# Graph layer 1 of a four-layer kernel: attention times tokens first, then times W

## The chip, the cores and the metric

The kernel runs on one core of one Trainium2 chip. The metric is the device time of one execution in microseconds (us), taken as the median over the runs. The core has four engines that compute and run side by side: TensorE (PE in the profile; its weight loads are PEld), VectorE (DVE), ScalarE (ACT) and GpSimd (POOL). SyncE (SP) issues the transfers. Every engine works through its own list of instructions in order and waits, by semaphores, for what it needs. All data are 32-bit floats unless said otherwise.

## The reference, cut to what matters

There are 64 graphs of 256 nodes with 256 features each, `x` of 64 x 256 x 256, and an adjacency matrix `adj` of 0 and 1 for each graph. Four layers follow one another; each normalises its input, applies ReLU, runs one kind of graph layer, and adds the outcome to `x`. Layer 0 is attention with eight heads, layer 2 three steps of a gated recurrent unit, layer 3 graph attention with four heads. The change is in layer 1, a graph attention with one head whose softmax runs over the rows (axis 1):

```python
h = jnp.maximum(_layernorm(x, axis=-1), 0.0)
Wh = jnp.einsum('bnf,fo->bno', h, W)
a1 = a[:fout, 0]
a2 = a[fout:, 0]
f1 = Wh @ a1
f2 = Wh @ a2
e = f1[:, :, None] + f2[:, None, :]
e = jnp.where(e >= 0, e, ALPHA * e)
attention = jnp.where(attn_mask > 0, e, MASK_FILL)
attention = jax.nn.softmax(attention, axis=1)
h_prime = jnp.einsum('bij,bjo->bio', attention, Wh)
x = x + jax.nn.elu(h_prime)
```

Two identities are used below: `attention @ (h @ W)` equals `(attention @ h) @ W`, and `(h @ W) @ a1` equals `h @ (W @ a1)`.

## The kernel before, in words

**Tiling.** Two graphs make a pair, so there are 32 pairs. A pair's `x` is one tile of 128 partitions by 4 x 256: the four token tiles `t` (two for each graph `g`) stand behind each other in a partition. Large working tiles have the tag `w4`, half as long ones `w2`, the eight accumulator banks `ps`; `part` are tiles of 512 elements for layer 2, and `mask` holds masks in bf16. A name in the profile such as `w` or `ps` is the tag without its number.

**Order.** The code of the layers does not issue instructions. It describes tasks with `add(...)`: on which engine (or on which of two), for how many us by the writer's estimate, which tiles are read and written, and the code to issue. `Plan.order` (lines 135 to 220) then goes through all tasks of all pairs and picks, again and again, the one that can begin first by those estimates. Ties are settled by a key: the pair's number times `PERIOD`, plus a number from the table `KEYS` by stage and engine (line 150). It also gives out the buffers; each tag has a count and a number of spares in `SLOTS` (line 265), and a task of a pair other than the oldest may not take the last spares. So several pairs are under way at once, and one pair's matrix products fill the time in which another pair waits. Products that use a part of the array ("rows", "columns", "halves") are kept together where possible. The outcome is a fixed order on each engine.

**Normalisation.** `norm_relu_T` (line 517) takes statistics on VectorE (L525, L527), the inverse root on GpSimd (L538, L539), and normalises four token tiles with ScalarE (L552) or VectorE (L558). It then turns the result with eight 128x128 transposes on TensorE (L577), four to a bank, and evicts each bank with ReLU, on ScalarE (L589) or VectorE (L590). The turned tile `hT` has features on the partitions. Layer 2 also needs the tokens upright, so it applies ReLU before the transposes, always on ScalarE.

**Layer 1** (`layer1`, line 834). The matrix `w1a` holds W and, in two more columns, W times the two halves of `a` (made once in `weights1`, line 395, with eight records at L406). For each token tile two products of 258 columns (L848) give `Wh` and both scores; VectorE copies the two score columns to `f12` (L852) and ScalarE the rest to `wh` (L855). `to_all` (line 813) transposes the f1 column to a row (L817), stores it and loads it into all partitions. ScalarE adds f2 and applies the leaky ReLU (L863); VectorE adds the mask, which a transfer has turned (L871), and takes the row's extreme (L688); ScalarE takes exp with its sum (L890). `wh` is divided by the sums (L896 or L900), and the products L913 of `e` with `wh`, 256 columns wide, give the outcome. ELU and the addition to `x` follow (L925 to L935). A product of 32-bit floats in the code is two records, each a weight load and a matmul, in the profile.

**Around it.** Layer 2's 24 gate products of 512 columns for each step (L1010) take most of TensorE's time. Its three message steps use `part` tiles: two masks are kept for the pair (L945), and each message product (L987) reads a high part (L971, L972) and a low part (L977). The fused mask row `lowered` (L688) is used by layers 0, 1 and 3. `evict` (L354 on ScalarE, L355 on VectorE) copies a bank to a tile. `turn` (L642) and `turn_chunks` (L663) turn tiles through a VectorE transpose of 32x32 blocks and transfers; the latter is used after each step of layer 2 for all pairs but the last.

Of the kernel before, what the change touches and what calls it, by code (L numbers as in the profile page):

```python
# [9 lines left out]
FP = mybir.dt.float32  # L10
# [29 lines left out]
class Plan:  # L40
# [18 lines left out]

    PERIOD = 1901  # L60


    KEYS = {
        ("io", "SP"): -29236, ("w", "SP"): 6718, ("w", "on"): -18369, ("w", "PE"): 8658, ("0n", "on"): -3731,
        ("0n", "SP"): 6915, ("0n", "PE"): 4357, ("0", "on"): 15591, ("0", "PE"): -6774, ("0s", "PE"): -16165,
        ("0s", "on"): 28734, ("0e", "on"): 12526, ("0e", "SP"): 43331, ("0c", "PE"): -12002, ("0c", "on"): 78735,
        ("1n", "on"): 783, ("1n", "SP"): -19498, ("1n", "PE"): -22885, ("1", "on"): -14680, ("1", "PE"): -13623,
        ("1r", "PE"): -1967, ("1r", "on"): -21520, ("1r", "SP"): -32647, ("1e", "on"): 1478, ("1c", "PE"): -9889,
        ("1c", "on"): -20145, ("2n", "on"): -1930, ("2n", "SP"): 38894, ("2n", "PE"): 5230, ("2", "on"): -6722,
        ("2h", "PE"): 9451, ("2h", "on"): -282, ("2m", "on"): -7288, ("2m", "PE"): 3883, ("2r", "PE"): 8501,  # L70
        ("2r", "on"): -21450, ("2u", "PE"): 9616, ("2u", "on"): 5167, ("2z", "PE"): 9836, ("2z", "on"): -13574,
        ("2b", "on"): 6539, ("2b", "SP"): 9757, ("3n", "on"): 23011, ("3n", "SP"): 30321, ("3n", "PE"): -1821,
        ("3", "on"): -11142, ("3", "PE"): -62749, ("3r", "on"): -37804, ("3r", "PE"): -7201, ("3r", "SP"): 18532,
        ("3e", "on"): 30365, ("3e", "SP"): 3733, ("3c", "PE"): 856, ("3c", "on"): 16925, ("3b", "on"): -30583,
        ("3b", "SP"): 12452, ("out", "SP"): -66168, ("2b", "PE"): 67575, ("3e", "PE"): -99949, ("3b", "PE"): 59983,
    }
# [147 lines left out]
def tile_adj_preln_d4(  # L224
# [42 lines left out]
        "w4": (24, [P, T * D], FP, 5),  # L267
        "part": (12, [P, N2], FR, 0),
        "f3": (2, [P, T, E3], FP, 0),
        "mask": (5, [P, T * N], BF, 0),  # L270
        "ps": (8, [P, 512], FP, 2),
        "w2": (3, [P, N2], FP, 2),
        "st": (4, [P, T, 6], FP, 1),
        "mv": (4, [P, T, 2], FP, 0),
        "rs": (4, [P, 2, T], FP, 2),
        "mx": (16, [P, H0], FP, 5),
        "zs": (12, [P, H0], FP, 7),
        "rz": (12, [P, H0], FP, 1),
        "f12": (2, [P, 2, T], FP, 1),
        "rows": (3, [T * H3, P], FP, 1),  # L280
        "dst": (4, [P, T, H3], FP, 3),
        "turn": (8, [P, T * N], FP, 3),
        "turn2": (4, [P, N2], FP, 1),
        "row1": (4, [N2], FP, 0),
        "row3": (4, [H3 * N2], FP, 3),
    }
# [10 lines left out]
    def held(name, shape):  # L297
        return const.tile(shape, FP, name=name)

    wq_sb, wk_sb, wv_sb, wo_sb = [held(name, [P, 2, D]) for name in ("wq_sb", "wk_sb", "wv_sb", "wo_sb")]  # L300
    bo_bc = held("bo_bc", [P, D])
    w1a = held("w1a", [P, 2, D + 2])
    w3a = held("w3a", [P, 2, E3])
# [91 lines left out]
    def weights1():  # L395

        load_w(w1a[:, :, 0:D], w1, W1)
        load(lambda: a1_sb.rearrange("p w k -> p (w k)"), a1.rearrange("(c p) e -> p (c e)", p=P), (W1, "a"))
        w1T = w4()
        turned(lambda o: w1a[:, o, 0:D], (0, 1), (0, 1), lambda: w1T()[:, 0:N2], (W1, w1T, [w1T]))  # L400
        ps = bank()

        def product():
            for f in range(2):
                for k in range(2):
                    mm(  # L406
                        ps()[:, 2 * f : 2 * f + 2], w1T()[:, k * D + f * P : k * D + (f + 1) * P], a1_sb[:, :, k],
                        start=k == 0, stop=k == 1,
                    )

        add((PE, 0.5, product), reads=[w1T, W1], writes=[ps])
        add(
            (V, 0.1, lambda: nc.vector.tensor_copy(w1a[:, :, D : D + 2], ps()[:, 0:4].rearrange("p (f w) -> p f w", w=2))),
            reads=[ps], writes=[W1],
        )

# [94 lines left out]


    def by_dma(l, p):

        return p < B // 2 - 1

    def norm_relu_T(xt, p, tokens=False):

# [29 lines left out]
        for g in range(2):  # L548
# [16 lines left out]
            else:  # L565
                forms = [(V, 0.7, scaled_v, True), (A, 1.0, lambda f=scaled: f(AF.Identity))]
            add(forms, reads=[(xt, g), (mv, g), (rs, g)], writes=[(xn, g)])
        hT = w4()
        hT.fine = fine
# [29 lines left out]

    def wide(hT, k):  # L600
        return tok(hT(), N2)[:, k]

    def graph_mm(ps, src, rhs, g, ):
# [53 lines left out]
    def turn_chunks(src, dst):  # L657
# [12 lines left out]
        dst.mixed = True  # L670

    def by_block(ap):
        return ap.rearrange("p (b n) -> p b n", b=4)
# [27 lines left out]
    def layer0(xt, p):  # L701
        at, hT = norm_relu_T(xt, p)
        mb = buf("mask")
# [130 lines left out]
    def layer1(xt, p):  # L834
        at, hT = norm_relu_T(xt, p)
        m1 = buf("mask")
        add(
            (V, dve2(T * N), lambda: nc.vector.tensor_scalar(
                m1(), at().bitcast(I32), 0.0, MASKED, ALU.is_le, ALU.mult), True),
            reads=[at, hT], writes=[m1],  # L840
        )
        wh, f12 = w4(), buf("f12")
        for t in range(T):
            ps = bank()

            def product(t=t, ps=ps):
                for k in range(2):
                    mm(ps()[:, 0 : D + 2], chunk(hT, k, t), w1a[:, k, :], start=k == 0, stop=k == 1)  # L848

            add((PE, 0.88, product), reads=[hT, W1], writes=[ps], claims=[wh, f12])  # L850
            add(
                (V, 0.07, lambda t=t, ps=ps: nc.vector.tensor_copy(f12()[:, :, t], ps()[:, D : D + 2])),  # L852
                reads=[ps], writes=[(f12, t)],
            )
            add((A, act(D), lambda t=t, ps=ps: nc.scalar.copy(tok(wh())[:, t, :], ps()[:, 0:D])), reads=[ps], writes=[(wh, t)])  # L855
        f1 = buf("w2")
        plan.stage = "1r"
        to_all(buf("row1"), f12, lambda: f12()[:, 0], T, [f1])
        e = w4()
        for t in range(T):  # L860
# [15 lines left out]
        for g in range(2):  # L876
# [17 lines left out]
            def divided(g=g):  # L894
                for t in (2 * g, 2 * g + 1):
                    nc.scalar.mul(tok(wh())[:, t, :], tok(wh())[:, t, :], rz()[:, t : t + 1])  # L896

            add(
                [
                    (V, dve(N2), lambda two=two: nc.vector.tensor_tensor(  # L900
                        tok(wh())[:, two, :], tok(wh())[:, two, :], rz()[:, two].unsqueeze(2).to_broadcast([P, 2, D]), ALU.mult), True),
                    (A, 2 * act(N, 1), divided),
                ],
                reads=[(rz, g)], writes=[(wh, 2 * g), (wh, 2 * g + 1)],
            )
        plan.stage = "1c"
        for g in range(2):
            ps, ex = bank(), buf("w2")

            def product(g=g, ps=ps):  # L910
                for ci in range(2):
                    for cj in range(2):
                        mm(  # L913
                            ps()[:, ci * D : (ci + 1) * D],
                            tok(e(), N)[:, 2 * g + cj, ci * P : (ci + 1) * P],
                            tok(wh())[:, 2 * g + cj, :],
                            start=cj == 0,
                            stop=cj == 1,
                        )

            parts = [(b, 2 * g + c) for b in (e, wh) for c in range(2)]
            add((PE, 1.76, product), reads=parts, writes=[ps], claims=[ex])

# [16 lines left out]
    def layer2(xt, p):  # L940
        at, hT, h = norm_relu_T(xt, p, tokens=True)
        ams = [buf("part") for g in range(2)]
# [56 lines left out]
        for l in range(NL):  # L999
# [44 lines left out]
            for o in range(2):  # L1044
                ps = gate(1.72, ((giT[:, l], aT),), (4 + o) * P, o, [u])
                add(
                    (V, dve(N2), lambda o=o, ps=ps, hn=hn: nc.vector.tensor_add(at_o(hn, o), ps(), at_o(hn, o))),  # L1047
                    reads=[ps], writes=[(hn, o)],
                )
                add(  # L1050
                    (A, act(N2, 1), lambda o=o, hn=hn: nc.scalar.activation(  # L1051
                        at_o(hn, o), at_o(hn, o), AF.Tanh, bias=bih_sb[:, 4 + o : 5 + o])),
                    writes=[(hn, o)],
                )
                add(
                    either(0.0, lambda eng, o=o, u=u, hT=hT, hn=hn: eng.tensor_sub(at_o(u, o), at_o(hT, o), at_o(hn, o))),  # L1056
                    reads=[(hT, o), (hn, o)], writes=[(u, o)],
                )
# [21 lines left out]
            plan.stage = "2b"  # L1080
            if by_dma(l, p):
                turn_chunks(u, h)
# [24 lines left out]
    def layer3(xt, p):  # L1107
        at, hT = norm_relu_T(xt, p)
        mb = buf("mask")
# [192 lines left out]
```

## Time and profile before

| | |
|---|---|
| median of 3 runs | 3577.19 us (3577.04 to 3578.66) |
| the profiled execution | 3574.28 us, its span 3572.5 us |
| TensorE busy | 3520.7 us |
| VectorE busy | 2802.2 us |
| ScalarE busy | 2614.9 us |
| GpSimd busy | 454.3 us |
| granted TensorE clock, mean | 0.995 |
| transfers | 687.72 MB, 193 GB/s |

A row of a group names the line, the engine, the operation, what is written and read with its shape, and the count; behind the bar stand the busy time of the group, the mean time of one in ns, and the idle time of the engine just before these instructions with what ended it. Matmuls overlap and their ends are modelled: a mean of 277 ns is not what one costs in a row of many, which is read from the starts in a listing by time. A row of waits gives the total in us, how often, and the longest.

### The profile page before, as it was taken

The numbers are of one execution on the slowest core, as the hardware profiler recorded it, in microseconds if no ns is written. First come the engines' busy times: TensorE is split into PE (matmuls) and PEld (weight loads), VectorE is DVE, ScalarE is ACT, GpSimd is POOL, SyncE is SP. The second block draws the span as 40 slices with busy tenths as digits, with TensorE's granted clock in tenths as the row PEclk, the third lists the DMA queues.
The fourth block names the chain that finished last, engine by engine and source line by source line (L and its number), as shares of the span: only waits on it lengthen the run. The fifth ranks groups of instructions, "written<-read, shape, count | busy, mean of one in ns | idle before, by whom it ended". The sixth has DMA issues, their size and how long they took to land.

```text
span 3572.5 us, 54870 instructions
## 1 busy us (share of the span) xinstructions
PE 3520.7 (99%) x15601; PEld 1990.1 (56%) x15601; DVE 2802.2 (78%) x8499; ACT 2614.9 (73%) x7012; POOL 454.3 (13%) x509
## 2 busy tenths in 40 slices
PE   8999999999999999999999999999999999999997
PEld 5565555555555555555555555555555555555554
DVE  7887687887778887788877878877888778878665
ACT  7796476877777777777867767876788767878555
POOL 2001111101111110111101111111111111111000
PEclk9999999999999999999999999999999999999998
DMA  8774487776767767677667767667687676786633
GB/s 232 205 207 133 130 235 202 205 197 181 207 183 221 207 180 200 190 220 201 195 183 196 223 183 212 190 191 212 180 224 199 180 198 187 210 223 180 169 107 118
DMA packets 544144, 687.72 MB, mean 193 GB/s; under 512 B 86113, under 2 KB 463073, under 8 KB 543841
## 3 DMA queue, kind: packets, MB, share of 16 engines
q1 hardware_dynamic: 543840, 684.21, 68.3%
q8 instruction: 125, 2.05, 0.3%
q14 instruction: 179, 1.46, 0.1%
HBM read 394.28 MB, written 281.35 MB: 189 GB/s over the span
## 4 chain that ended last, share of the span: by engine, by line
PE 82%; ACT 7%; DVE 6%; DMA 3%; issue 1%; SPq 1%; POOL 1%; DVEq 0%; ACTq 0%; POOLq 0%
PE ps L1010 45%; PE ps L719 6%; PE ps L607 6%; PE ps L987 4%; PE ps L740 3%; PE ps L1128 3%; PE ps L848 3%; PE ps L577 3%; PE ps L1183 3%; PE ps L792 2%; PE ps L913 2%; ACT w L695 2%; ACT w L1160 1%; DVE w L642 1%; DMA x<-in_x_dram 1%; DVE w L688 1%
## 5 line engine op out<-in xcount | busy, mean ns | idle before, releaser
L1010 PE MATMUL ps<-w,whhT 128*128 128x512 f32 x2304 | 1076.7, 595 | 0.3 <-ACT w L354 0.2
L1010 PE MATMUL ps<-w,giT 128*128 128x512 f32 x2304 | 1070.9, 593 | 0.0
L695 ACT ACTIVATE w<-w,mx 128x256 f32<-128x256 f32 x1536 | 758.9, 499 | 18.5 <-DVE mx L688 17.9
L1010 PEld LDWEIGHTS ps<-w,giT 128*128 128x128 f32 x2304 | 434.0, 190 | 526.2 <-issue 509.9
L1010 PEld LDWEIGHTS ps<-w,whhT 128*128 128x128 f32 x2304 | 423.4, 190 | 454.5 <-issue 426.1
L354 ACT COPY w<-ps 128x512 f32<-128x512 f32 x519 | 291.1, 581 | 307.0 <-PE ps L719 90.6
L642 DVE STREAM_TRANSPOSE w<-w 128x1024 f32<-128x1024 f32 x380 | 469.6, 1236 | 43.6 <-ACT w L695 21.8
L688 DVE CUSTOM_DVE_ANT_0 w<-ps,mask 128x256 f32<-128x256 f32 x1024 | 370.6, 416 | 124.2 <-PE ps L740 124.0
L695 ACT ACTIVATION_READ_ACCUMULATOR w<-w,mx 128x1 f32 x1536 | 294.8, 192 | 0.0
L538 POOL TENSOR_SCALAR rs<-mv 128x4 f32<-128x4 f32 x129 | 41.2, 319 | 1973.8 <-DVE mv L527 1953.9
L772 ACT ACTIVATE w<-w,rz 128x256 f32<-128x256 f32 x606 | 266.2, 501 | 2.2 <-DVE rz L765 2.1
L552 ACT ACTIVATE w<-x,rs 128x256 f32<-128x256 f32 x396 | 208.1, 592 | 54.5 <-DVE rs L544 52.3
L1064 ACT ACTIVATE w<-ps,brz 128x512 f32<-128x512 f32 x192 | 129.9, 677 | 156.3 <-PE ps L1010 156.3
L1034 ACT ACTIVATE w<-ps,brz 128x512 f32<-128x512 f32 x192 | 130.1, 678 | 147.6 <-PE ps L1010 147.3
L987 PE MATMUL ps<-part,part 128*128 128x256 f32 x1536 | 222.2, 298 | 9.7 <-DVE part L945 4.9
L1056 POOL TENSOR_TENSOR w<-w,w 128x512 f32<-128x512 f32 x87 | 111.8, 1285 | 909.5 <-ACT w L1051 540.4
L1160 ACT ACTIVATE w<-w,f 128x256 f32<-128x256 f32 x512 | 220.3, 499 | 4.6 <-DMA w<-row 4.5
L987 PEld LDWEIGHTS ps<-part,part 128*128 128x128 f32 x1536 | 195.7, 193 | 42.0 <-issue 23.7
L1051 ACT ACTIVATE w<-w,bih_sb 128x512 f32<-128x512 f32 x192 | 136.4, 717 | 102.6 <-DVE w L1047 101.7
L525 DVE BATCH_NORM_STATS2 st<-x 128x6 f32<-128x256 f32 x512 | 189.7, 412 | 25.4 <-DMA x<-in_x_dram 23.5
L1069 DVE SCALAR_TENSOR_TENSOR w<-w,w 128x512 f32<-128x512 f32 x192 | 136.3, 710 | 92.3 <-ACT w L1064 90.3
L688 DVE CUSTOM_DVE_ANT_0 w<-w,mask 128x256 f32<-128x256 f32 x512 | 197.7, 426 | 8.5 <-ACT w L1160 8.2
(114 smaller groups left out, 5129.4 us busy)
## 6 DMA issues: line engine op xcount, KB each, us to landing
turn<-w SPq DMA_DIRECT2D x473, 512.0 KB
w<-turn SPq DMA_DIRECT2D x1892, 128.0 KB
w<-in_adj_dram SPq DMA_DIRECT2D x128, 512.0 KB
w<-row SPq DMA_DIRECT2D x64, 512.0 KB
x<-in_x_dram SPq DMA_DIRECT2D x64, 256.0 KB
out_dram<-x SPq DMA_DIRECT2D x64, 256.0 KB
turn<-w SPq DMA_DIRECT2D x62, 256.0 KB
w<-turn SPq DMA_DIRECT2D x248, 64.0 KB
```

The lines of the kernel that those rows point to most:

```text
L354: (A, act(n), lambda: nc.scalar.copy(dst(), src())),
L525: nc.vector.bn_stats(st()[:, t, :], tok(xt())[:, t, :])
L552: nc.scalar.activation(tok(xn())[:, t, :], tok(xt())[:, t, :], func, bias=rs()[:, 1, t : t + 1], scale=rs()[:, 0, t : t + 1])
L607: mm(ps()[:, c * D : (c + 1) * D], chunk(src, k, 2 * g + c), rhs[:, k, :], start=k == 0, stop=k == 1)
L642: add((V, dve(T * N), lambda: nc.vector.transpose(blocks(), blocks())), writes=[e])
L688: nc.vector.tensor_tensor_reduce(row, src, mask, scale, 3.0e38, ALU.add, ALU.min, mn)
L695: nc.scalar.activation(row(e, r), row(e, r), AF.Exp, bias=mn()[:, r : r + 1], scale=-1.0, accum_out=zs()[:, z0(r) : z0(r) + 1])
L719: mm(ps(), w[:, k, o * P : (o + 1) * P], wide(hT, k), start=k == 0, stop=k == 1)
L772: op(row, row, rz()[:, r : r + 1])
L987: mm(ps()[:, o * N : (o + 1) * N], chunk_of(part(), h.mixed, c, o), tok(ams[g](), N)[:, c, :], start=i == 0 and c == 0, stop=i == 1 and c ...
L1010: mm(ps(), w[:, k, c0 : c0 + P], wide(src, k), start=n == 0, stop=n == 2 * len(terms) - 1)
L1160: nc.scalar.activation(dst, src, AF.Prelu, bias=f()[:, t, D + h : D + h + 1], alpha=ALPHA)
```

## The change: what it does, and the diff

Layer 1 no longer turns its normalised tokens: the function, now `norm_relu`, stops after the normalisation with ReLU on ScalarE and returns upright tokens `h`. W times the halves of `a` is made once as two rows of 256, the same in all partitions (`wa_bc`); the scores are eight fused multiply-and-add rows for a pair on VectorE, which write `f12` directly and use `e` for their products. `h`, in place of `wh`, is divided by the sums of the softmax. The attention is multiplied with `h` first; that sum is evicted to `u`, and `u` is multiplied with W. ELU and the addition are as before. All keys, `PERIOD` and several counts of buffers and spares are new: `part` goes from 12 tiles to 10, `w2` from 3 to 4. `by_dma` is asked with a stage now; with `TURNED` as it stands it holds after each step of layer 2, as before, and for none of the four normalisations, so `turn_rows` is not called. The subtraction at L1056 reads and writes what it did.

```diff
-    PERIOD = 1901
+    PERIOD = 2008
     KEYS = {
-        ("io", "SP"): -29236, ("w", "SP"): 6718, ("w", "on"): -18369, ("w", "PE"): 8658, ("0n", "on"): -3731,
+        ("io", "SP"): -22628, ("w", "SP"): 6160, ("w", "on"): -16051, ("w", "PE"): 28184, ("0n", "on"): -19306,
...
-        "part": (12, [P, N2], FR, 0),
+        "part": (10, [P, N2], FR, 1),
-        "w2": (3, [P, N2], FP, 2),
+        "w2": (4, [P, N2], FP, 1),
...
-        add((PE, 0.5, product), reads=[w1T, W1], writes=[ps])
+        add((PE, 1.72, product), reads=[w1T, a_w], writes=[ps])
+        add(evict(N2, lambda: wa_bc.rearrange("p w f -> p (w f)"), ps), reads=[ps], writes=[(W1, "b")])
...
+    TURNED = ("2m",)
     def by_dma(l, p):
-        return p < B // 2 - 1
+        return l in TURNED and p < B // 2 - 1
...
+        if not turning:
+            plan.stage = base
+            return at, xn
...
     def layer1(xt, p):
-        at, hT = norm_relu_T(xt, p)
+        at, h = norm_relu(xt, p, tokens=True, turning=False)
...
-        wh, f12 = w4(), buf("f12")
-        for t in range(T):
-            ps = bank()
-            def product(t=t, ps=ps):
-                for k in range(2):
-                    mm(ps()[:, 0 : D + 2], chunk(hT, k, t), w1a[:, k, :], start=k == 0, stop=k == 1)
-            add((PE, 0.88, product), reads=[hT, W1], writes=[ps], claims=[wh, f12])
-            add(
-                (V, 0.07, lambda t=t, ps=ps: nc.vector.tensor_copy(f12()[:, :, t], ps()[:, D : D + 2])),
-                reads=[ps], writes=[(f12, t)],
-            )
-            add((A, act(D), lambda t=t, ps=ps: nc.scalar.copy(tok(wh())[:, t, :], ps()[:, 0:D])), reads=[ps], writes=[(wh, t)])
+        e, f12 = w4(), buf("f12")
+        for g in range(2):
+            def dots(g=g):
+                for t in (2 * g, 2 * g + 1):
+                    for w in range(2):
+                        nc.vector.tensor_tensor_reduce(
+                            tok(e(), N)[:, t, :], tok(h())[:, t, :], wa_bc[:, w, :], 1.0, 0.0, ALU.mult, ALU.add, f12()[:, w, t : t + 1])
+            add(
+                (V, 4 * FUSED, dots, True), reads=[(h, g), W1], writes=[(e, 2 * g), (e, 2 * g + 1), (f12, g)],
+            )
...
-            ps, ex = bank(), buf("w2")
-            def product(g=g, ps=ps):
-                for ci in range(2):
-                    for cj in range(2):
+            psu, ps, u, ex = bank(), bank(), buf("w2"), buf("w2")
+            def sums(g=g, psu=psu):
+                for k in range(2):
+                    for c in range(2):
                         mm(
-                            ps()[:, ci * D : (ci + 1) * D],
-                            tok(e(), N)[:, 2 * g + cj, ci * P : (ci + 1) * P],
-                            tok(wh())[:, 2 * g + cj, :],
-                            start=cj == 0,
-                            stop=cj == 1,
+                            psu()[:, k * N : (k + 1) * N],
+                            tok(h())[:, 2 * g + c, k * P : (k + 1) * P],
+                            tok(e(), N)[:, 2 * g + c, :],
+                            start=c == 0,
+                            stop=c == 1,
                         )
-            add((PE, 1.76, product), reads=parts, writes=[ps], claims=[ex])
+            add((PE, 1.74, sums), reads=[(h, g), (e, 2 * g), (e, 2 * g + 1)], writes=[psu], claims=[u])
+            add(evict(N2, u, psu), reads=[psu], writes=[u])
+            def product(u=u, ps=ps):
+                for c in range(2):
+                    for k in range(2):
+                        mm(
+                            ps()[:, c * D : (c + 1) * D], u()[:, k * N + c * P : k * N + (c + 1) * P], w1_sb[:, k, :],
+                            start=k == 0, stop=k == 1,
+                        )
+            add((PE, 1.74, product), reads=[u, W1], writes=[ps], claims=[ex])
```

## The prediction

> **What bounds the kernel now.** I read the busy table first, then TensorE's own waits, the chain that ended last, TensorE's order of work in time, and the costliest groups.
>
> ```profile
> span 3572.5 us, 54870 instructions
> PE 3520.7 (99%) x15601; PEld 1990.1 (56%) x15601; DVE 2802.2 (78%) x8499; ACT 2614.9 (73%) x7012; POOL 454.3 (13%) x509
> PE 82%; ACT 7%; DVE 6%; DMA 3%; issue 1%; SPq 1%; POOL 1%; DVEq 0%; ACTq 0%; POOLq 0%
> ```
>
> TensorE is busy for 3520.7 of 3572.5 us, so at most 51.8 us are idle. Asked for 637 to 3246 us alone (24 of the 32 pairs), the waits of TensorE are these and no others, 8.3 us together:
>
> ```profile
> PE ps L987 <- DVE part L945: 4.3, 6, 1.7
> PE ps L607 <- DVE w L355: 2.5, 2, 1.3
> PE ps L607 <- ACT w L354: 1.5, 6, 0.3
> ```
>
> Four pairs take 434.3 us there (the same place of the pattern begins at 1071.85 and at 1506.19 us), so 108.6 us a pair. The rest of the idle time lies at the ends: 8.7 + 0.9 + 3.6 us before 31 us, and 22.4 us of waits after 3400 us. TensorE's throughput is the bound; VectorE at 78% and ScalarE at 73% run beside it. A busy TensorE can still be slow inside, so I look at starts in the order of time, columns start, duration, operation, count:
>
> ```profile
> 1436.67 1.89 PE L913 MATMUL ps<-w,w 128*128 128x256 f32 x8
> 1438.39 1.88 PE L1010 MATMUL ps<-w,whhT 128*128 128x512 f32 x4
> ...
> 1474.30 1.04 PE L577 MATMUL ps<-ident,w 128*128 128x128 f32 x8
> 1475.17 1.88 PE L1010 MATMUL ps<-w,whhT 128*128 128x512 f32 x4
> ...
> 1500.43 3.75 PE L848 MATMUL ps<-w1a,w 128*128 128x258 f32 x16
> 1503.83 2.25 PE L987 MATMUL ps<-part,part 128*128 128x256 f32 x16
> ```
>
> Each group starts before the shown end of the one in front, because the ends are modelled. From start to start, eight transposes take 0.87 us, eight records of the attention product 1.72 us, sixteen of the product with W 3.40 us. One product in the code is two records.
>
> The groups that the edits touch, busy time and mean of one behind the bar:
>
> ```profile
> L577 PE MATMUL ps<-ident,w 128*128 128x128 f32 x1024 | 136.1, 277 | 14.6 <-ACT w L552 14.5
> L848 PE MATMUL ps<-w1a,w 128*128 128x258 f32 x512 | 118.0, 382 | 0.0
> L913 PE MATMUL ps<-w,w 128*128 128x256 f32 x512 | 121.4, 380 | 0.0
> L589 ACT ACTIVATE w<-ps 128x512 f32<-128x512 f32 x182 | 98.0, 596 | 12.1 <-PE ps L577 12.0
> L855 ACT COPY w<-ps 128x256 f32<-128x256 f32 x128 | 45.0, 371 | 30.2 <-DVE f L852 16.9 <-PE ps L848 13.3
> L852 DVE COPY f<-ps 128x2 f32<-128x2 f32 x128 | 18.9, 151 | 26.2 <-PE ps L848 20.7 <-ACT w L855 4.8
> ```
>
> **The change, part by part.** TensorE sets the end, so its parts count in full and those of the others count only as far as they delay it.
>
> *Transposes.* Layer 1 held 8 of the 32 transposes of a pair, 256 of the 1024 in the L577 row. Eight cost 0.87 us: 32 x 0.87 = 27.8 us removed. Eight behind a product in small tiles take 0.93 (1457.53 to 1458.46 us), which would make 29.8; I take 0.87, the usual case. [...] But the eight starts span 0.87 us, 109 ns each, at a granted clock of 1.00; only that is given back.
>
> *Products.* Before: 4 token tiles x 2 = 8 with W (3.40 us) and 8 with the attention (2 x 1.72). After: 8 for normalised tokens times attention, 8 for that times W, all 256 columns wide. Counting every eight records at 1.72 gives 6.88 against 6.84 us, +1.3 us in 32 pairs; counting columns (256 for 258, in sixteen records) gives 3.40 x 2/258 = 0.03 less, -0.9 us. I take 0. The exchange of the order of multiplication saves no product.
>
> *Weights, once.* The product of a with W becomes 4 products of 256 columns (1.72 us) for 8 records of 2 columns; these ran from 37.06 to 37.88 us, 0.82, so +0.9 us. VectorE gains one broadcast copy of 512 elements (0.68 us, the L355 row's 677 ns) and ScalarE or VectorE one eviction, both inside the first 100 us beside the other weights. At worst all lies on the path, +2 us.
>
> *The new score sums.* Eight fused multiply-and-add rows of 256 a pair on VectorE. The trace has no such form with two f32 inputs; the nearest is the fused mask row:
>
> ```profile
> 1496.69 0.42 DVE L688 CUSTOM_DVE_ANT_0 w<-ps,mask 128x256 f32<-128x256 f32 x1 [0.36 <-PE ps L740]
> 1497.04 0.08 DVE L688 DVE_READ_ACCUMULATOR2_ANT mx<- 128x1 f32 x1
> 1497.04 0.42 DVE L688 CUSTOM_DVE_ANT_0 w<-ps,mask 128x256 f32<-128x256 f32 x1
> 1497.38 0.08 DVE L688 DVE_READ_ACCUMULATOR2_ANT mx<- 128x1 f32 x1
> ```
>
> From start to start it takes 0.345 us: 8 x 32 x 0.345 = 88 us of VectorE. [...] The rows above overlap, so 0.345; the bounds are 88 and 128. VectorE loses four f12 copies a pair (18.9 us), its share of layer-1 normalisation, which ReLU now ties to ScalarE (116 of the 384 calls of layers 0, 1 and 3 ran on VectorE; a third, 39, at 0.36: 14 us) and one or two ReLU evictions. It comes to 2802 + 88 - 18.9 - 14 = 2857, at most 2897, plus up to 64 x 0.68 = 43 us if it takes the new evictions: 80 to 83% of the new span. The cover is TensorE's own 107.7 us a pair. Were it gone, the 2.76 us a pair would fall on the path, +88 us.
>
> *ScalarE.* Removed: 128 W evictions (45.0 us) and nearly all of 64 transposed ReLU evictions (64 x 0.596 = 38). Added: up to 64 evictions of the new sum (0.581 each, 37 us) and the 39 normalisation calls (208.1/396 = 0.53, 21 us). Net about -25 us of 2615: hidden on an engine with a quarter of its time free, worth nothing by itself.
>
> *Waits moved.* VectorE's score sums wait for the normalised tokens from ScalarE, where the f12 copies waited for L848. Behind them in VectorE's order stand mask rows, which release the score banks, and L977, which feeds L987. The row of f1 goes to the SyncE queue after the sums; its eviction, one store and one load are unchanged in number and size, as is the mask's turned load, but all transfers queued behind that store wait with it. VectorE's free 20 us a pair cover it. Then the attention sum is evicted before the product with W: 0.58 us plus the way there, twice a pair. TensorE has other pairs' work to put between; if nothing were put there, 64 x 0.6 = 38 us. The nearest row, L607 behind the evicted context, waited 4.0 us in 24 pairs, so I take 0 and keep +10 as the bound.
>
> *Code that is added but not reached.* The normalisation asks whether its layer is turned by transfers; only the hidden state of layer 2 is, and was before. No cost.
>
> *Order and buffers.* Every key and some slot counts are new. Part falls from 12 to 10, w2 rises from 3 to 4, and layer 1 holds two large tiles fewer. In steady work there is 8.3 us to win; at the ends some 35. Leaving or entering a product in small tiles costs 0.09 us (L607 from 1407.15 to 1408.97 us takes 1.82, not 1.72-1.73): one switch in or out more or fewer a pair moves 3 us, two sides of one tile group 6. So the order is worth -12 to +8 us; I take 0.
>
> **Sum.** -27.8 + 0 + 0.9 = -26.9 us. The profiled execution took 3574.28 us, of which 1.8 lie around the span; the sum gives 3547.4 there. Its time is 2.9 us under the median of 3577.19, so the forecast for a median is 3577.19 - 26.9 = 3550 us, 0.75% faster.
>
> **Rivals.** *Slower, by the part buffers.* Layer 2 keeps two for the mask of a pair and uses two for each of its six message products. With two pairs in layer 2, four are held; of 10, six are left for high and low parts, three products deep instead of four. If L977 and L971 come late, L987 waits: it waited 9.7 us in 13 places, 0.75 us each. There are 6 x 32 = 192 message products. From 27 / 0.75 = 36 further waits the gain is gone; if half of the 192 waited, +72 us, 3550 + 72 = 3622 us. For it: L987 has most of the steady waits. Against it: VectorE and ScalarE are a fifth free.
>
> *Part of the gain is lost in new waits* before the product with W or before the f1 row: 0.2 to 0.5 us a pair, 3557 to 3566 us. Against it: a pair now lacks no other work to put there.
>
> *No gain*, if VectorE becomes the bound where its work bunches: it would need another 20 us a pair, while at most (2897 + 43 - 2802) / 32 = 4.3 come. About 3577 us.
>
> *More gain*: the order also shortens the ends or merges tile groups, 12 us: 3538 us.
>
> **How the numbers follow.** Main case 0.70, 3550 us (3543 to 3556). More gain 0.13, partial gain 0.10, no gain 0.03, slower 0.04. A measurement tells about 0.2%, 7 us, from no change: faster 0.93, same 0.03, slower 0.04. The 8-in-10 range leaves out the last two cases and the outer ends of the gain cases, 3536 to 3563 us.
>
> **What would show it.** L577 with about 768 records and unchanged spacing; the two new products 512 records each, eight in 1.72 us; no row for the W eviction or for the f12 copies; 256 more fused VectorE rows near 0.42 us; VectorE at 80 to 83%; TensorE still at 98 to 99% and a four-pair period of 434.3 - 4 x 0.87 = 430.8 us. Wrong would be a TensorE with several us a pair of waits for part, for the evicted sum or for the f1 row, a fused row well over 0.5 us, or a period that fell by more than 5 us, which would say that the order carried more than the edit.

## The result, and the profile after

The changed kernel takes 3548.87 us (3547.27 to 3552.61), the kernel before 3577.11 us beside it: 28.2 us less, ratio 0.9922, 95% interval 0.9909 to 0.9935. The forecast was 3550 us. The profiled execution of the changed kernel took 3550.16 us, its span 3548.4.

The busy table and the chain that ended last, of the kernel after:

```profile
span 3548.4 us, 54621 instructions
PE 3500.6 (99%) x15345; PEld 1965.5 (55%) x15345; DVE 2879.5 (81%) x8769; ACT 2634.5 (74%) x7011; POOL 452.0 (13%) x505
PE 89%; DVE 4%; ACT 3%; DMA 2%; SPq 1%; issue 1%; POOL 0%; DVEq 0%; ACTq 0%; POOLq 0%
```

TensorE is busy for 20 us less and has 256 records fewer, the transposes. VectorE gained 77 us and ScalarE 20, and the kernel became faster all the same. TensorE's waits from 637 to 3246 us were three rows and 8.3 us; now they are this row and no other (total, times, longest):

```profile
PE ps L1059 <- DVE w L1125: 1.5, 2, 0.7
```

The waits over the whole span fell from 47.0 to 42.9 us, nearly all at the two ends. Two stretches of four pairs in the middle, columns start and length, busy time of TensorE, its weight loads, VectorE, ScalarE and GpSimd, then the granted clock, the share of the transfers and their GB/s:

```profile
1418.05:1848.67 430.62, 430.62 (x1897) 241.38 (x1897) 360.00 (x1098) 327.59 (x875) 56.15 (x62) 1.00 0.66 201
1848.67:2279.31 430.64, 430.64 (x1898) 241.41 (x1897) 359.59 (x1098) 327.46 (x875) 56.19 (x62) 1.00 0.65 201
```

Four pairs took 434.3 us; now 430.6, which is 0.93 us a pair less. The groups that answer to those shown of before:

```profile
L602 PE MATMUL ps<-ident,w 128*128 128x128 f32 x768 | 104.0, 278 | 12.8 <-ACT w L557 12.7
L966 PE MATMUL ps<-w_sb,w 128*128 128x256 f32 x512 | 118.8, 382 | 0.0
L952 PE MATMUL ps<-w,w 128*128 128x256 f32 x512 | 118.2, 383 | 3.2 <-ACT w L935 2.1 <-ACT w L737 0.8 <-DVE rz L807 0.3
L614 ACT ACTIVATE w<-ps 128x512 f32<-128x512 f32 x120 | 65.0, 592 | 10.8 <-PE ps L602 10.8
L890 DVE CUSTOM_DVE_ANT_0 w<-w,wa_bc 128x256 f32<-128x256 f32 x256 | 101.8, 421 | 5.5 <-DMA w<-turn 1.1
```

The transposes went from 1024 to 768. The two products, attention times tokens (L952) and that times W (L966), are busy for 237.0 us together where L848 and L913 were for 239.4. The rows for the eviction of W's product and for the f12 copies are gone.

L966 shows no idle time before it, but this hides a wait, because the modelled ends of the matmuls cover it. In eight pairs of the 32, one in four in the middle, the products with W stand directly behind the attention sums, and their weight loads (PEld) wait for the evicted sum. One such place (rows of other work left out):

```profile
1078.40 3.62 PE L952 MATMUL ps<-w,w 128*128 128x256 f32 x16
1082.01 1.59 PEld L966 LDWEIGHTS ps<-w_sb,w 128*128 128x128 f32 x8 [0.39 <-ACT w L355]
1082.01 3.98 PE L966 MATMUL ps<-w_sb,w 128*128 128x256 f32 x16
1084.00 1.59 PEld L966 LDWEIGHTS ps<-w_sb,w 128*128 128x128 f32 x8 [0.40 <-DVE w L356]
1085.83 0.59 PE L1059 MATMUL ps<-w,whhT 128*128 128x512 f32 x1
```

From 1078.40 to 1085.83 us the 32 records take 7.43 us, where two times sixteen take 6.90 elsewhere. The weight loads of L966 waited 6.1 us for the evicted sum in all; the later starts cost TensorE 3.8 us, which count as busy.

### The profile page after: what moved, and what is told of

The parts are those of the page before. It is cut to its first block, busy times and chain, and to the rows that moved or that the text cites. A ratio compares the mean times of both kernels' runs of the same rounds, so it can differ in the third digit from the quotient of the medians.

```text
span 3548.4 us, 54621 instructions
## 1 busy us (share of the span) xinstructions
PE 3500.6 (99%) x15345; PEld 1965.5 (55%) x15345; DVE 2879.5 (81%) x8769; ACT 2634.5 (74%) x7011; POOL 452.0 (13%) x505
## 4 chain that ended last, share of the span: by engine, by line
PE 89%; DVE 4%; ACT 3%; DMA 2%; SPq 1%; issue 1%; POOL 0%; DVEq 0%; ACTq 0%; POOLq 0%
PE ps L1059 50%; PE ps L761 6%; PE ps L637 6%; PE ps L1036 5%; PE ps L782 4%; PE ps L1234 3%; PE ps L1179 3%; PE ps L834 3%; PE ps L966 3%; PE ps L952 3%; PE ps L602 2%; ACT w L737 1%; DVE w L730 1%; DVE w L672 1%; DMA x<-in_x_dram 1%
## 5 line engine op out<-in xcount | busy, mean ns | idle before, releaser
L355 ACT COPY w<-ps 128x512 f32<-128x512 f32 x574 | 324.4, 581 | 275.1 <-PE ps L761 102.3
L814 ACT ACTIVATE w<-w,rz 128x256 f32<-128x256 f32 x672 | 292.8, 503 | 5.8 <-DVE rz L807 5.5
L557 ACT ACTIVATE w<-x,rs 128x256 f32<-128x256 f32 x466 | 245.0, 591 | 50.3 <-DVE rs L549 50.1
L1036 PE MATMUL ps<-part,part 128*128 128x256 f32 x1536 | 226.0, 299 | 2.1 <-ACT part L1020 1.5
L1036 PEld LDWEIGHTS ps<-part,part 128*128 128x128 f32 x1536 | 196.1, 191 | 35.6 <-issue 20.1
L1088 DVE SCALAR_TENSOR_TENSOR w<-w,w 128x512 f32<-128x512 f32 x192 | 136.4, 711 | 87.2 <-ACT w L1069 45.5
L1120 DVE SCALAR_TENSOR_TENSOR w<-w,w 128x512 f32<-128x512 f32 x192 | 141.5, 737 | 80.0 <-ACT w L1115 68.1
```

The lines of the kernel that those rows point to most:

```text
L355: (A, act(n), lambda: nc.scalar.copy(dst(), src())),
L557: nc.scalar.activation(tok(xn())[:, t, :], tok(xt())[:, t, :], func, bias=rs()[:, 1, t : t + 1], scale=rs()[:, 0, t : t + 1])
L814: op(row, row, rz()[:, r : r + 1])
L1036: mm(ps()[:, o * N : (o + 1) * N], chunk_of(part(), h.mixed, c, o), tok(ams[g](), N)[:, c, :], start=i == 0 and c == 0, stop=i == 1 and c ...
```

## The experiments

The theory: 256 transposes cost TensorE 109 ns each and are the whole gain, the rest is hidden, the order is worth nothing. The rivals: the gain is the order's; a transpose costs the 277 ns of its group's mean (L577 before); VectorE's added work is not hidden. Every ratio is to the kernel before, run beside the experiment, where it took 3576.03 to 3577.25 us. Differences from the kernel after compare runs taken apart, and are uncertain by about 1 us more than the intervals say.

### Parts of the change alone, with the order made by the plan as it falls

**The kernel before, with the order tables and the counts of buffers of the kernel after.**

```diff
-    PERIOD = 1901
+    PERIOD = 2008
...
-        "part": (12, [P, N2], FR, 0),
+        "part": (10, [P, N2], FR, 1),
...
```

> The kernel before with the keys, the period and the slot counts of the kernel after; layer 1 as before. If the removed transposes carry the gain: 3577 us, within 7. If the new order carries it: 3549 to 3556 us. Stages of layer 1 that the new table no longer names get no offset.

Measured: 3662.43 us, ratio 1.0241 (1.0227 to 1.0255).

**The kernel after, with the keys and the period of the kernel before.**

```diff
-    PERIOD = 2008
+    PERIOD = 1901
...
-        ("io", "SP"): -22628, ("w", "SP"): 6160, ("w", "on"): -16051, ("w", "PE"): 28184, ("0n", "on"): -19306,
+        ("io", "SP"): -29236, ("w", "SP"): 6718, ("w", "on"): -18369, ("w", "PE"): 8658, ("0n", "on"): -3731,
```

> The kernel after with the keys and the period of the kernel before, slot counts as after. If the edit of layer 1 carries the gain: 3549 us, within 7. If the new order carries it or the edit needs it: 3565 us or more.

Measured: 3606.2 us, ratio 1.0082 (1.0068 to 1.0095).

**Transposes put back into the kernel after, as tasks of their own.**

```diff
+        for i in range(2):
+            ps = bank()
+            def turn(i=i, ps=ps):
+                for t in range(T):
+                    nc.tensor.transpose(ps()[:, t * P : (t + 1) * P], tok(h())[:, t, i * P : (i + 1) * P], ident)
+            add((PE, 4 * TURN, turn), reads=[h], writes=[ps])
```

> The kernel after with eight transposes a pair of layer 1's tokens put back on TensorE, into two banks that nothing reads. Throughput, 109 ns each: 3549 + 28 = 3577 us. [...] If they find idle time: 3549 to 3555 us.

Measured: 3649.05 us, ratio 1.0206 (1.0192 to 1.022).

**Transposes left out of the kernel before.**

```diff
-        at, hT = norm_relu_T(xt, p)
+        at, hT = norm_relu_T(xt, p, turning=False)
...
+        if not turning:
+            for i in range(2):
+                dst, src = lambda i=i: tok(hT(), N2)[:, i, :], lambda i=i: tok(xn(), N2)[:, i, :]
```

> The kernel before with layer 1's eight transposes left out and the ReLU copying the upright tokens instead (two copies of 512 elements a pair); the products with W then multiply tokens that were never turned, so layer 1's values change and nothing else. Transposes alone carry the gain: 3577 - 28 = 3549 us. If reordering the two products or the score sums have a share of it: 3556 us or more.

Measured: 3588.01 us, ratio 1.0034 (1.0021 to 1.0047): slower than before with less to do.

All four miss what the theory gave, by 39 to 86 us, in one direction. What they share is that each changed the tasks or the keys without making keys for that set of tasks. The first has the same tasks as the kernel before (its counts of buffers differ too) and takes 86 us more; TensorE's waits are 96.3 us there instead of 47.0, and it is busy for 3557.1 instead of 3520.7 us. So these four say nothing on the transposes, but much on the order: with a table that was not made for its tasks the same work takes up to 2.4% longer. The second exceeds the kernel before by 30 us: under the old table the edit of layer 1 is worth less than nothing.

### The same questions with every instruction in its place

Here the order is kept: apart from the instructions named, each engine has the same list as the kernel it is made from.

**Eight transposes a pair in the kernel after, four in front of each attention sum, in its bank.**

```diff
             def sums(g=g, psu=psu):
+                for j in range(4):
+                    nc.tensor.transpose(psu()[:, j * P : (j + 1) * P], tok(h())[:, 2 * g + j // 2, j % 2 * P : (j % 2 + 1) * P], ident)
                 for k in range(2):
```

> The kernel after, every instruction in its order, with eight transposes a pair more on TensorE: four directly in front of each attention sum, into the sum's own bank, which the sum then overwrites. Throughput, 109 ns each: 3549 + 28 = 3577 us. [...] If they fall into free time: 3549 to 3555 us.

Measured: 3567.78 us, ratio 0.9978 (0.997 to 0.9986), 18.9 us above the kernel after (20.0 us by the two ratios). The inserted transposes are L951 in its list by time:

```profile
1869.86 0.60 PE L951 MATMUL ps<-ident,w 128*128 128x128 f32 x4
1870.29 1.89 PE L954 MATMUL ps<-w,w 128*128 128x256 f32 x8
1872.02 0.60 PE L951 MATMUL ps<-ident,w 128*128 128x128 f32 x4
1872.46 1.89 PE L954 MATMUL ps<-w,w 128*128 128x256 f32 x8
```

Four take 0.43 to 0.44 us from start to start, 108 to 109 ns each as reckoned, and eight records of the sum still take 1.73 us. But four pairs take 433.6 us, 2.95 us more and not 4 x 0.87 = 3.48. The missing 0.53 us is the late start of L966 shown above, once in four pairs: the transposes in front of the second sum give the first one's eviction time, and the product with W takes its 3.45 us there too. Over the whole run the inserted transposes add 27.7 us where they stand; 3.8 us come back at L966 and 4.1 us in other places, part of them the waits, which fell from 42.9 to 39.7 us.

**The kernel before with layer 1's transposes not issued.**

```diff
+            if base == "1":
+                turn = lambda: None
             add((PE, 4 * TURN, turn), reads=[(xn, i) if fine else xn], writes=[ps], claims=[hT])
...
+            if base == "1":
+                src = lambda i=i: tok(xn(), N2)[:, i, :]
```

> The kernel before, every instruction in its order, with layer 1's 256 transposes not issued; the ReLU that evicted them reads the upright tokens, so layer 1's values change and nothing else. If the transposes are the whole gain: 3577 - 28 = 3549 us. If the exchanged products, the score sums or the new order have a share of it: 3556 us or more. If these cost something: under 3542 us.

Measured: 3556.05 us, ratio 0.9947 (0.9935 to 0.996), 20.0 us under the kernel before. The profiled execution was the slowest of the five: its span is 15.1 us under that of before. In it the 32 groups of eight free 28.7 us where they stood (0.87 us in most pairs, 0.93 in seven), and 13.2 us come back elsewhere, most of it at L607 behind the evicted context (4.1), L817 behind the f1 column (4.1) and L740 (2.4). The waits, which rose from 47.0 to 51.6 us, show about a third of this; the rest are later starts under the modelled ends, as at L966.

The two runs bracket the step from both ends and agree: 256 transposes are worth 19 to 20 us of the end, 74 to 78 ns each, with some 5 us of uncertainty that leaves out both the 27.8 us of the forecast and the 71 us that 256 times the group's mean of 277 ns would make. The transposes themselves take the 108 to 109 ns of their starts; a part of what they free goes into waits for the other engines.

**Each score sum computed twice, and four times, in the kernel after.**

```diff
-                    for w in range(2):
+                    for w in (0, 1) * 2:
```

> The kernel after in its order, with each of the eight score sums of a pair computed twice: 88 us more of VectorE, 81% to 84%. Hidden: 3549 us, within 5. On the path in full: 3637 us.

> The kernel after in its order, with each score sum computed four times: 265 us more of VectorE, 81% to about 89%. Cover still whole: 3549 to 3556 us. Cover gone in places where VectorE's work bunches: 3560 to 3650 us. On the path in full: 3814 us.

The second run has `* 4` in place of `* 2`. Measured: 3628.36 us (ratio 1.0149, 1.0135 to 1.0163) and 3883.44 us (1.0861, 1.0846 to 1.0876): 79.5 and 334.6 us above the kernel after. VectorE's busy time rose by 106.9 and 332.0 us, so as much as 74% of the doubled sums, and all of the quadrupled ones, came out at the end, on an engine that was idle for 19% of the span. Of TensorE's waits from 637 to 3246 us, 37.8 us in five rows, these three are the largest in the run with the sums doubled:

```profile
PE ps L859 <- DVE dst L1192: 15.6, 6, 2.6
PE ps L859 <- DVE f L890: 11.0, 6, 1.9
PE ps L1036 <- DVE part L1026: 7.9, 9, 1.1
```

L859 is the small transpose that turns the f1 column, or layer 3's, to a row. It stands at a place in TensorE's list where VectorE had the column ready before. Now TensorE waits there for the sums, or for layer 3's scores that stand behind sums in VectorE's list, and all of TensorE's later work waits with it.

Not all of the loss is waiting. With the sums doubled the span grew by 77.2 us: 57.0 of waits, and 20.0 of busy time of TensorE for the same records. With four sums it grew by 330.7: 266.3 and 64.6. The granted clock fell with it, from 0.994 to 0.990 and 0.957. One place in the run with four sums: a wait of TensorE in the listing by time, then the stretch from 1548.1 to 1558.3 us, with the granted clock third from the end:

```profile
1551.86 1.65 PE L1036 MATMUL ps<-part,part 128*128 128x256 f32 x6 [7.86 <-DVE part L1026]
...
1548.10:1558.30 10.20, 6.44 (x35) 4.82 (x37) 9.14 (x38) 3.18 (x11) 0.00 (x0) 0.50 0.60 182
```

The clock was 1.00 up to 1548 us and again from 1558.3. So the agreement of 334.6 us at the end with 332.0 us of VectorE is in part chance.

### Orders made for the tasks

For these four the keys, the period and the spares were varied at random, and the set was kept whose plan ended earliest by the estimates that the tasks carry; the counts of buffers stayed.

**The kernel after with such a further order.**

```diff
-        "ps": (8, [P, 512], FP, 2),
+        "ps": (8, [P, 512], FP, 1),
...
-        "w2": (4, [P, N2], FP, 1),
+        "w2": (4, [P, N2], FP, 0),
```

The diff names two of the spares; keys and period differ too.

> The kernel after with no change but a further order: other keys, another period and other spares. If the order of the kernel after is as good as such orders get: 3549 us, within 7. If there is more to win by order alone: 3530 to 3542 us. If an order is only good by luck on this chip: 3556 us or more.

Measured: 3583.48 us, ratio 1.0018 (1.0009 to 1.0027), 34.6 us above the kernel after with the same tasks. The plan gave VectorE 43 us and ScalarE 25 us more, but TensorE's busy time is 3500.3 us, the same as the kernel after's 3500.6; all of the difference is waits, 76.4 instead of 42.9 us. From 637 to 3246 us they are:

```profile
PE ps L637 <- DVE w L356: 25.1, 12, 2.2
PE ps L1036 <- DVE part L994: 6.7, 8, 0.8
PE ps L1036 <- ACT w L737: 3.1, 4, 0.8
```

L637 is the product behind an evicted context; in the kernel after TensorE does not wait there. How the order of the kernel after was found is not on record, so this shows how far two orders can lie apart, not how far orders found alike do.

**Each score sum twice, with the doubled cost in the task.**

```diff
-                    for w in range(2):
+                    for w in (0, 1) * 2:
...
-                (V, 4 * FUSED, dots, True), reads=[(h, g), W1], writes=[(e, 2 * g), (e, 2 * g + 1), (f12, g)],
+                (V, 8 * FUSED, dots, True), reads=[(h, g), W1], writes=[(e, 2 * g), (e, 2 * g + 1), (f12, g)],
```

> Each score sum computed twice, as in the run before with 88 us more of VectorE, but with the doubled cost written into the task and an order made for it in the same way as for the kernel after with a further order. If VectorE's free time is real and only the order must know the work: within 7 us of that kernel. If VectorE's added time is on the path whatever the order: 80 us above it, 3620 to 3630 us.

Measured: 3557.91 us, ratio 0.9947 (0.9934 to 0.9959). It is 25.6 us faster than the kernel after with a further order, so the expectation of "within 7 us" missed, downward, because that order turned out poor. The comparison that holds is with the same doubled sums in the kept order: 3628.36 against 3557.91 us, 70 us less for the same tasks, and 9 us above the kernel after with 125 us more of VectorE (3004.3 against 2879.5). Its waits from 637 to 3246 us are 9.3 us, where the kept order had 37.8:

```profile
PE ps L859 <- DVE f L890: 8.4, 14, 0.7
PE ps L859 <- ACT w L355: 0.7, 1, 0.7
PE ps L859 <- DVE dst L1192: 0.2, 1, 0.2
```

VectorE's free time is real, and here it covered work that the order was made for. This is one order: whether another, made without the written cost, would also have covered the sums was not tried. But 70 us is twice what the two orders of the kernel after differ by.

**Eight transposes a pair put back, with an order made for them.** The edit is that of the earlier run with tasks of their own.

> Eight transposes a pair put back on TensorE into two banks of their own that nothing reads, with an order made for it in the same way. Throughput, 109 ns each: 28 us above the kernel after with a further order. Partly in idle time, as with the order kept: 19 us above it. [...] If transposes never cost anything but an unlucky order: within 7 us of it.

Measured: 3590.1 us, ratio 1.0039 (1.0026 to 1.0051), 6.6 us above the kernel after with a further order and 41 us above the kernel after. With orders that differ by 35 us this is inconclusive on the transposes.

**Layers 2 and 3 taken off TensorE as well.**

```diff
-    TURNED = ("2m",)
+    TURNED = ("2m", "2", "3")
```

> The kernel after with the normalised tokens of layers 2 and 3 also taken off TensorE, for all pairs but the last: a VectorE transpose of 1024 elements and five transfers (1 MB) each in place of eight transposes and two evictions; order made for it. TensorE loses 31 x 16 x 0.109 = 54 us, VectorE gains 31 x 2 x 1.24 = 77 us. TensorE still the bound: 3500 to 3535 us. VectorE's or the transfers' lateness takes the gain: 3545 us or more.

Measured: 3548.08 us, ratio 0.9923 (0.9909 to 0.9936): the time of the kernel after, not better. The busy table of this run:

```profile
span 3546.6 us, 54130 instructions
PE 3460.7 (98%) x14849; PEld 1917.7 (54%) x14849; DVE 2950.6 (83%) x8846; ACT 2609.4 (74%) x6951; POOL 440.9 (12%) x482
```

TensorE lost 496 transposes and 39.9 us of busy time, and its waits rose from 42.9 to 76.4 us, by 33.5. The gain turned into waits, most of them for VectorE (L1036 for its part tiles, 20.0 us; L859 for the score sums, 6.6). Whether another order would bring it out was not tried.

## Why the prediction was right, point by point

**The bound.** Right for the ordered kernel: TensorE has 1.5 us of waits in the middle, and the period of four pairs, forecast at 430.8 us, is 430.6. It was too simple as a rule for other changes. A VectorE with 19% free time set the end as soon as its work came where the order didn't expect it.

**The transposes.** The place and the price per start were right; that all of it reaches the end was not. The step counted 27.8 us; the two runs with the order kept measured 20.0 and 18.9. The transposes do take 27.7 and 28.7 us where they stand, and the rest is what TensorE then waits for, at L966 in the one run, at L607, L817 and L740 in the other. The mean of 277 ns in the group's row of before (L577) misleads as a price: 256 x 0.277 = 71 us is excluded by both.

**The products.** Right: sixteen records take 3.45 us both for the sums (1858.81 to 1862.26) and for the products with W (1865.70 to 1869.15), except where the evicted sum came late.

**The score sums.** The forecast of 80 to 83% for VectorE held, at 81%. The duration from start to start was read as 0.345 us from a row that is not quite like it: every second sum takes 0.46 to 0.47 us (last section), and doubling them added 106.9 us and not 88. The bound of 128 us for the sums, and with it the 2897 us of VectorE at most, was the author's estimate of 256 x (0.42 + 0.08) us, a row and its accumulator read one behind the other, with the durations of the L688 rows of before. No run shows the term: in the rows of the last section the sums start 0.35 and 0.46 to 0.47 us apart. The sentence that VectorE's free 20 us a pair cover them is true of the order that was made with them in it, and was wrongly argued from the idle share: with the order kept, 107 us more of VectorE cost 79.5.

**ScalarE.** Forecast 25 us less, measured 20 us more: the plan moved other work to it, 66 more of the divisions of layer 0 (606 to 672) and 70 more calls of the normalisation (396 to 466) where 39 were reckoned. Nothing shows that it cost time.

**The waits moved.** Nearly as forecast: the evicted sum costs 3.8 us at L966, where 0 was taken and 10 was the bound, and none of TensorE's matmuls waits at L859 for the f1 row. What would have made the step wrong was also named rightly, for the f1 row is what the doubled sums waited for.

**The rival of the part buffers** is out for this order: with ten tiles L1036 waits 1.9 us, where L987 waited 9.7 with twelve.

**The order.** Here the prediction was lucky. It took 0, between -12 and +8 us. Beside the 20.0 us of the transposes, all the rest of the change, order, exchange, sums and weights, brought 3556.05 - 3548.87 = 7.2 us of gain, where 0.9 us of loss was reckoned. TensorE's busy time in these two runs is the same, 3500.8 and 3500.6 us, and its waits are 51.6 and 42.9: this gain is waits that the kernel after does not have. So two terms missed in opposite directions, the transposes by 8 us and the rest by 8, and the sum came out right. The 7 us lie inside the bound, but the reason given for it, that only 8 us of steady waits and a switch of tile groups were at stake, does not hold for orders in general: a second order of the kernel after lost 34.6 us, the other kernel's table cost the kernel after 57 us and the kernel before 86. Whether the new keys, or the tasks that the exchange moved, saved these waits stays open.

## What to carry to other kernels

In a kernel whose lists of instructions are planned in advance, an engine's idle share is no cover by itself: here added work was hidden where the order was made with its cost, and most of it came out at the end where it was not. Price an operation on the bounding engine by the starts of a long row, not by the mean of its group, and then expect a part of even that to go into waits for other engines. A busy bounding engine can hold such waits: read the starts of what follows, and the waits of its weight loads. To test one part, keep every other instruction in its place, since a plan made anew moves more than the part is worth.

## What the runs showed of the hardware that had not been expected

The fused sums come in two speeds. In the kernel after, on VectorE by start and duration (the 0.08 us rows that read each sum's accumulator are left out):

```profile
1170.80 0.42 DVE L890 CUSTOM_DVE_ANT_0 w<-w,wa_bc 128x256 f32<-128x256 f32 x1
1171.26 0.42 DVE L890 CUSTOM_DVE_ANT_0 w<-w,wa_bc 128x256 f32<-128x256 f32 x1
1171.61 0.42 DVE L890 CUSTOM_DVE_ANT_0 w<-w,wa_bc 128x256 f32<-128x256 f32 x1
1172.08 0.42 DVE L890 CUSTOM_DVE_ANT_0 w<-w,wa_bc 128x256 f32<-128x256 f32 x1
```

The first and the second sum write the same row of `e`, and the second starts 0.46 us behind the first; the third writes another row and starts 0.35 us behind the second; the fourth again writes the third's row, 0.47 us. With the sums computed four times over, where all eight of a token tile write one row, they follow at 0.46 to 0.47 us:

```profile
1291.75 0.42 DVE L890 CUSTOM_DVE_ANT_0 w<-w,wa_bc 128x256 f32<-128x256 f32 x1
1292.21 0.42 DVE L890 CUSTOM_DVE_ANT_0 w<-w,wa_bc 128x256 f32<-128x256 f32 x1
1292.68 0.42 DVE L890 CUSTOM_DVE_ANT_0 w<-w,wa_bc 128x256 f32<-128x256 f32 x1
```

So 0.12 us more goes with a product written over the row just written. Such a sum also reads the same row of `h` again, and which of the two is the cause was not tried. Taking the two token tiles of a graph in turn would tell whether it is either; by an estimate from these starts it would then save 128 x 0.12 = 15 us of VectorE.
